# A neighbour mask and layernorm steps moved from VectorE to ScalarE in a four-layer graph kernel

## The chip, the core and the metric

The kernel runs on one core of a Trainium2 chip. A core has five engines that work side by side, each with its own list of instructions, which it takes in order: TensorE (PE; its weight loads are PEld), VectorE (DVE), ScalarE (ACT), GpSimd (POOL) and SyncE (SP). They wait for one another through semaphores. The metric is the device time of one execution in microseconds (us), the median over several runs. A profile is one execution that the hardware profiler recorded.

## The reference

Sixteen graphs of 1024 nodes with 64 features each pass through four layers. Each layer normalizes the features, clips them at zero, computes something over the graph, and adds the result to `x`:

```python
h = jnp.maximum(_layernorm(x, axis=-1), 0.0)   # (x - mean) / sqrt(var + 1e-5), per node over 64 features
x = x + layer(h, adj)                          # four times, with four different layers
```

- Layer 0: `messages = adj @ h`, then `tanh([h, messages] @ W1 + b1) @ W2 + b2`.
- Layer 1: `((adj + I) @ h) / rowsum(adj + I)`.
- Layer 2: a node's neighbours are the columns with `adj > 0`, without itself. Where there are more than ten, some are struck out by a rule on their rank. Over the neighbours that remain (and the node itself) the 25, 50 and 75% quantiles are taken in each feature, weighted 0.25, 0.5, 0.25 and added to `h`; two matrix products with a Relu follow, and the node mask.
- Layer 3: `(adj @ h) / degree @ W_n + h @ W_s + bias`.

The adjacency is not negative: an entry is zero or between 0.05 and 1.

## The kernel before

Nodes lie 128 to a tile, eight tiles to a graph (`NB = 8`, `C = 64`, `P = 128`). A graph's work is cut into six streams, Python generators that emit instructions piece by piece:

- `adjacency` (from L863): for each of eight row blocks it takes a block `a` of 128 x 1024 float32 that was loaded three blocks ahead, makes the mask `nb` (L874: 1 where `a > 0`) and clears its diagonal (L876), transposes `a` on TensorE into `adjt` (L881, copied out by ScalarE at L882), and counts the neighbours of each row on ScalarE, by a pass over `nb` with an accumulator output (L887). Then it makes keys for the neighbours that remain (L895 to L956), writes them to DRAM, and orders the nodes by their number of neighbours (L958 to L1004).
- `layers`: layers 0 and 1, and layer 2's layernorm, whose result goes to DRAM as `h_d`.
- `neighbour_lists`: the keys come back in the new order of nodes by indirect DMAs from GpSimd (L1019), and VectorE draws the neighbours' numbers out, eight at a time, with MAX8 (L1034, L1048).
- `gathers`: for each neighbour place and each block of nodes one indirect DMA from GpSimd fetches 128 rows of `h_d` (L1165), 152 a graph. The blocks form five groups with their own buffers.
- `sorts`: VectorE sorts each group's gathered rows by a network of minima and maxima (L1208), one `tensor_tensor` each, and adds up the weighted quantiles (L1229, L1231).
- `tail`: eight indirect DMAs from GpSimd (L1251) fetch the sums in the old order; then come layer 2's products and layer 3.

The order is set when the program is built. A planner keeps a `Clock` with an estimated time for VectorE, TensorE, ScalarE and GpSimd. Each stream advances it with the estimated costs of what it emitted (`after(dve, pe, act)`) and yields the time from which it wants to go on. The loop at the end takes the first stream in a fixed order of priority whose time has come. So the estimates decide how the streams' instructions interleave, and every engine then executes that order as it stands. A new graph's `adjacency` begins once the previous one's keys are done and `adjt` is no longer needed. A group's gathers wait until the same group of the previous graph is sorted, and the sorts wait for the gathers.

The layernorm `preln` is called four times per graph, 64 times in all: three times from `layers`, once from `tail`. It takes the sum of the 64 features on VectorE (L816), scales it to the mean (L817), subtracts it (L818), squares on ScalarE (L819), sums the squares on VectorE (L821), takes the root on ScalarE (L822) and the reciprocal on VectorE (L824), multiplies (L825), and writes the clipped result on ScalarE (L826). The operations over the features treat all eight blocks, 512 elements per partition, in one instruction. The three yields let other streams' instructions in between.

Of the kernel before, what the change touches and what calls it, by code (L numbers as in the profile page):

```python
# [7 lines left out]
F32 = mybir.dt.float32  # L8
# [5 lines left out]
AF = mybir.ActivationFunctionType  # L14
ALU = mybir.AluOpType
AX = mybir.AxisListType

P = 128
C = 64
NB = 8  # L20
# [689 lines left out]
def direct_path(ctx: ExitStack, tc: tile.TileContext, t: dict, out: bass.AP, flag):  # L710
# [3 lines left out]
    nc = tc.nc  # L714
# [6 lines left out]
    nodes = ctx.enter_context(tc.tile_pool(name="nodes", bufs=2))  # L721
# [6 lines left out]
    tt, ts, act = nc.vector.tensor_tensor, nc.vector.tensor_scalar, nc.scalar.activation  # L728
# [55 lines left out]
    clk = Clock()  # L784

    def after(dve=0.0, pe=0.0, act=0.0, lat=0.3):

        clk.dve += dve
        at = clk.dve
        if pe:  # L790
            clk.pe = at = max(clk.pe, at) + pe
        if act:
            clk.act = at = max(clk.act, at) + act
        return at + lat


    def bank(dt=F32):
        return psum.tile([P, 2048 // mybir.dt.size(dt)], dt, tag="t", name="pt", bufs=3)
# [8 lines left out]
    def mid(u, shape):  # L807

        return work.tile(shape, F32, tag=f"mid{u}", name="mid", bufs=2)

    def preln(u, x, ha):

        s = nodes.tile([P, 4, NB], F32, name="stat")
        xc = mid(u, [P, NB, C])
        sq = mid(u, [P, NB, C])
        nc.vector.tensor_reduce(s[:, 0], x, AX.X, ALU.add)  # L816
        ts(s[:, 1], s[:, 0], 1.0 / C, None, op0=ALU.mult)  # L817
        tt(xc, x, s[:, 1, :, None].to_broadcast([P, NB, C]), ALU.subtract)  # L818
        act(sq, xc, AF.Square)  # L819
        yield after(1.5, act=0.65)  # L820
        nc.vector.tensor_reduce(s[:, 2], sq, AX.X, ALU.add)  # L821
        act(s[:, 3], s[:, 2], AF.Sqrt, bias=eps, scale=1.0 / C)  # L822
        yield after(0.7, act=1.0)
        nc.vector.reciprocal(s[:, 2], s[:, 3])  # L824
        tt(xc, xc, s[:, 2, :, None].to_broadcast([P, NB, C]), ALU.mult)  # L825
        act(ha[:, :, :C], xc, AF.Relu)  # L826
        yield after(0.9, act=0.65)

    def transposed(h, dst):

# [28 lines left out]
    def load_rows(k):  # L859

        if k < B * NB:
            a = loads.tile([P, N], F32, name="a", bufs=3)
            nc.sync.dma_start(a, adj[k // NB, k % NB * P:(k % NB + 1) * P, :])  # L863
            queued.append(a)


    def adjacency(b):
        g = state[b]
        adjt = graph.tile([P, NB, N], F32, name="adjt")
        nb = graph.tile([P, NB, N], F16, name="nb")  # L870
        mn = nodes.tile([P, 3, NB], F32, name="mn")
        for i in range(NB):
            a = queued.pop(0)
            ts(nb[:, i, :], a, 0.0, None, op0=ALU.is_gt)  # L874
            d = slice(i * P, (i + 1) * P)
            tt(nb[:, i, d], nb[:, i, d], offdiag, ALU.mult)  # L876
            for q in range(2):
                p = bank()
                for u in range(4):
                    j = 4 * q + u  # L880
                    nc.tensor.transpose(p[:, u * P:(u + 1) * P], a[:, j * P:(j + 1) * P], identf)  # L881
                nc.scalar.copy(adjt[:, 4 * q:4 * q + 4, i * P:(i + 1) * P],  # L882
                               p.rearrange("p (u m) -> p u m", m=P))
            load_rows(NB * b + i + 3)
            for q in range(2):
                s = slice(q * 512, (q + 1) * 512)
                act(nb[:, i, s], nb[:, i, s], AF.Copy, accum_out=mn[:, q, i:i + 1])  # L887
            yield max(after(0.9, pe=2.2, act=2.9) - 3.0, clk.dve + 3.1)
        g.update(adjt=adjt, at=clk.act)
        done.add(("rows", b))  # L890

# [24 lines left out]
        for i in range(NB):  # L916
# [8 lines left out]
            for q in range(2):  # L925
                s = slice(q * 512, (q + 1) * 512)
# [3 lines left out]
            if waiting:  # L930
                yield waiting[2]
                ts(gone[:, waiting[0], :], waiting[1], sf[:, 1, waiting[0]:waiting[0] + 1], -1.0,  # L932
                   op0=ALU.is_equal, op1=ALU.mult)
# [4 lines left out]
           op0=ALU.is_equal, op1=ALU.mult)  # L938
# [3 lines left out]
        for i in range(NB):  # L942

            p = bank2()
            for q in range(2):
                s = slice(q * 512, (q + 1) * 512)
# [143 lines left out]
    def layers(b):  # L1090
# [4 lines left out]
        yield max(g["at"], clk.dve + 3)  # L1095
        ha = nodes.tile([P, NB, C + 1], F32, name="ha")
        yield from preln(0, x, ha)
        zt = big(0, [P, N])
        transposed(ha, zt[:C])
# [11 lines left out]
        clk.dve += 0.7  # L1111
        ha = nodes.tile([P, NB, C + 1], F32, name="ha")
        yield from preln(0, x, ha)

        nc.vector.memset(ha[:, :, C:], 1.0)  # L1115
# [23 lines left out]
        clk.dve += 2.4  # L1139
        ha = nodes.tile([P, NB, C + 1], F32, name="h2", bufs=3)  # L1140
        yield from preln(0, x, ha)
        nc.sync.dma_start(h_ds[b % 3][:N].rearrange("(i p) c -> p i c", p=P), ha[:, :, :C])
        ts(deg[:, 1], deg[:, 0], 0.0, None, op0=ALU.is_equal)
# [178 lines left out]
    def over_graphs(step, *needs):  # L1322
# [5 lines left out]

    streams = [
        over_graphs(adjacency, ("adjt", 1), ("keys", 1), ("sorts", 3)),  # L1330
        over_graphs(layers, ("rows", 0), ("tail", 3)),
        over_graphs(tail, ("sorts", 0)),
# [142 lines left out]
```

## Time and profile before

| | before |
|---|---|
| time, median of 3 runs | 5551.11 us (5551.11 to 5564.75) |
| span of the profiled execution | 4044.6 us |
| VectorE busy | 3476.7 us, 86% of the span |
| GpSimd busy | 2951.5 us, 73% |
| TensorE busy | 2039.3 us, 50% |
| ScalarE busy | 1411.8 us, 35% |
| granted TensorE clock | 0.698 of full speed |

The profiled execution is shorter than the timed ones by 1507 us, although the program and its inputs are the same. So the profile shows in which way the engines wait for one another, while its lengths can't simply be carried over to the timed runs.

In the profile, "busy" is the time in which an engine executes an instruction that isn't mere control. A group's line gives the source line, the engine, the operation, what is written and read, the number of instructions, the busy time in us and the mean of one in ns, and behind the second bar the idle time of the engine just ahead of these instructions with what ended it. "issue" there means that the profile shows nothing that the engine waited for.

### The profile page before, as it was taken

How to read it: one execution, taken by the hardware profiler on the slowest of the kernel's cores; microseconds unless marked ns; L12 is line 12 of the kernel's file. 1: busy time of each engine (PE TensorE's matmuls, PEld its weight loads, DVE VectorE, ACT ScalarE, POOL GpSimd, SP SyncE). 2: the span in 40 equal slices, each digit the busy share in tenths (PEclk: the TensorE clock that was granted, in tenths of full speed). 3: DMA queues.
4: the chain of work that ended last, by engine and by line, in shares of the span. 5: the costliest groups of instructions: out<-in, count | busy, mean ns of one | idle time of the engine just before them, and what ended most of it. 6: DMA issues, size and time to landing. Idle time of an engine off the chain costs nothing.

```text
span 4044.6 us, 34028 instructions
## 1 busy us (share of the span) xinstructions
PE 2039.3 (50%) x8387; PEld 980.5 (24%) x8387; DVE 3476.7 (86%) x9450; ACT 1411.8 (35%) x2594; POOL 2951.5 (73%) x2707
## 2 busy tenths in 40 slices
PE   7565574264735546473554647455454745540303
PEld 3223231121313122231322213132221313110101
DVE  2649998997999999998998989899998999997583
ACT  6544442342425333342533434253432424320000
POOL 0277777777777777777777777777777777777771
PEclk8676676576767767776675767677677776765656
DMA  2343543444434454543444444443535444442312
GB/s 88 115 87 88 120 111 53 110 92 90 117 55 126 86 120 94 109 104 50 125 90 115 94 96 114 53 138 74 130 83 105 108 62 112 76 109 37 68 26 53
DMA packets 251857, 372.57 MB, mean 92 GB/s; under 512 B 120160, under 2 KB 120352, under 8 KB 251648
## 3 DMA queue, kind: packets, MB, share of 16 engines
q0 software_dynamic: 92640, 117.88, 23.5%
q1 hardware_dynamic: 158864, 251.87, 18.4%
q8 instruction: 68, 1.11, 0.1%
q14 instruction: 141, 1.16, 0.1%
q10 hardware_dynamic: 144, 0.56, 0.0%
HBM read 256.84 MB, written 113.25 MB: 92 GB/s over the span
## 4 chain that ended last, share of the span: by engine, by line
POOL 41%; DVE 33%; issue 13%; PE 5%; DMA 5%; ACT 2%; DVEq 0%; POOLq 0%; ACTq 0%
POOL raw L1165 37%; DVE other L1208 8%; DVE raw L1208 7%; DVE most L1048 5%; PE pt L845 4%; POOL res L1251 3%; DMA raw<-h_d,index 2%; DVE found L1034 2%; DVE agg L1231 2%; DVE k L1045 1%; DMA k<-keys_d,node 1%; DVE found L1050 1%; DVE k L1043 1%; ACT adjt L1125 1%; DVE nb L874 1%
## 5 line engine op out<-in xcount | busy, mean ns | idle before, releaser
L1165 POOL DMA_INDIRECT raw<-h_d,index x2432 | 2666.0, 1096 | 757.5 <-issue 724.7
L1208 DVE TENSOR_TENSOR other<-raw 128x128 f32<-128x128 f32 (+7 forms) x1488 | 766.5, 533 | 73.4 <-DMA raw<-h_d,index 60.3
L1208 DVE TENSOR_TENSOR raw<-other 128x256 f32<-128x256 f32 (+10 forms) x1424 | 679.1, 490 | 4.3
L845 PE MATMUL pt<-adjt,ha 128*65 128x512 f32 (+1 forms) x1024 | 492.9, 644 | 299.3 <-DVE ha L1115 299.2
L881 PE MATMUL pt<-ef,a 128*128 128x128 f32 x1024 | 232.7, 391 | 389.4 <-ACT adjt L882 354.5
L1295 PE MATMUL tm<-at,ha 128*64 128x512 f32 x512 | 286.0, 677 | 54.9 <-DMA at<-adjt_d 52.4
L845 PEld LDWEIGHTS pt<-adjt,ha 128*65 128x65 f32 (+1 forms) x1024 | 150.0, 150 | 621.9 <-issue 569.6
L1048 DVE MAX8 most<-k 128x8 uint16<-128x1024 uint16 x224 | 275.0, 1228 | 7.7
L881 PEld LDWEIGHTS pt<-ef,a 128*128 128x128 f32 x1024 | 173.5, 203 | 441.8 <-ACT adjt L882 391.0
L922 PE MATMUL pt<-eh,nbt 128*128 128x512 f16 (+3 forms) x1024 | 210.0, 364 | 125.9 <-ACT nbt L911 125.4
L1019 POOL DMA_INDIRECT k<-keys_d,node x128 | 131.0, 1023 | 191.2 <-DVE node L1004 122.0
L956 ACT ACTIVATE nb<-pt 128x1024 f16<-128x1024 f32 x128 | 130.8, 1022 | 390.2 <-PE pt L952 248.3
L834 PE MATMUL pt<-ef,res 128*64 128x128 f32 x128 | 30.2, 418 | 425.7 <-DVE res L1255 335.3
L1034 DVE MAX8 found<-k 128x8 f32<-128x1024 f16 x128 | 156.3, 1221 | 99.2 <-DMA k<-keys_d,node 99.2
L887 ACT ACTIVATE nb<-nb 128x512 f16<-128x512 f16 x256 | 159.6, 628 | 206.2 <-DVE nb L876 119.4
L978 ACT ACTIVATE sink<-pt,neg 128x1024 f16<-128x1024 f32 x128 | 140.4, 1121 | 244.9 <-PE pt L973 244.9
L1208 DVE TENSOR_TENSOR other<-raw,other 128x256 f32<-128x256 f32 (+4 forms) x592 | 206.9, 354 | 5.4
L846 ACT COPY big<-pt 64x1024 f32<-64x1024 f32 (+1 forms) x32 | 32.2, 1007 | 505.9 <-PE pt L845 505.9
L1251 POOL DMA_INDIRECT res<-agg_d,pos x128 | 146.1, 1141 | 83.5 <-DMA agg_d<-agg 43.0
L927 ACT ACTIVATE ab<-pt,sf 128x512 f16<-128x512 f32 x256 | 161.8, 687 | 124.6 <-DVE gone L932 67.8
L1208 DVE TENSOR_TENSOR raw<-raw,other 128x256 f32<-128x256 f32 (+3 forms) x608 | 203.0, 338 | 0.0
L1208 DVE TENSOR_TENSOR raw<-other,raw 128x128 f32<-128x128 f32 (+5 forms) x560 | 196.1, 357 | 3.1
(154 smaller groups left out, 4068.0 us busy)
## 6 DMA issues: line engine op xcount, KB each, us to landing
a<-in_adj_dram SPq DMA_DIRECT2D x128, 512.0 KB, 3.6
adjt_d<-adjt SPq DMA_DIRECT2D x128, 512.0 KB, 5.7
at<-adjt_d SPq DMA_DIRECT2D x256, 256.0 KB, 3.8
raw<-h_d,index POOLq DMA_INDIRECT x2432
keys_d<-nb SPq DMA_DIRECT2D x128, 256.0 KB, 2.3
x<-in_x_dram SPq DMA_DIRECT2D x16, 256.0 KB, 2.9
h_d<-h SPq DMA_DIRECT2D x16, 256.0 KB, 4.2
agg_d<-agg SPq DMA_DIRECT2D x16, 256.0 KB, 2.8
```

Source lines behind the costliest of these rows:

```text
L845: nc.tensor.matmul(p[p0:p0 + n, s], h[:, j, :n], adjt[:, j, s], start=j == 0, stop=j == NB - 1)
L881: nc.tensor.transpose(p[:, u * P:(u + 1) * P], a[:, j * P:(j + 1) * P], identf)
L887: act(nb[:, i, s], nb[:, i, s], AF.Copy, accum_out=mn[:, q, i:i + 1])
L922: nc.tensor.matmul(p[:, o:e], nbt[:, j, :], stair[:, :e - o], start=j % 4 == 0, stop=j % 4 == 3)
L927: act(ab[:, s], p[:, s], AF.Abs, bias=sf[:, 2 + q, i:i + 1], scale=2.0)
L978: act(sink, p, AF.Sign, bias=neg[:, i:i + 1], accum_out=over[:, i:i + 1])
L1034: nc.vector.max(out=found[:, o:o + 8], in_=src)
L1048: nc.vector.max(out=most, in_=less.bitcast(U16))
L1165: nc.gpsimd.indirect_dma_start(raw[:, s, i * C:(i + 1) * C], None, h_ds[b % 3], bass.IndirectOffsetOnAxis(ap=g["index"][:, at:at + 1], axi ...
L1208: tt(to, v0, v1, ALU.max if greater else ALU.min)
L1251: nc.gpsimd.indirect_dma_start(res[:, i, :], None, g["agg_d"], bass.IndirectOffsetOnAxis(ap=g["pos"][:, i:i + 1], axis=0))
L1295: nc.tensor.matmul(p[:C, :], ha[:, j, :C], ats[k], start=j == 0, stop=j == NB - 1)
```

## The change

The mask is made by ScalarE's `Sign` in place of VectorE's comparison. The row sums are taken with `Relu` in place of `Copy`, so that an entry below zero, of which `Sign` makes -1, counts as no neighbour. In the layernorm the mean's negative goes as a bias column into ScalarE's `Square`, and the sum of squares comes out of the same instruction's accumulator; the last step is one `Relu` with a scale and a bias column. A column is one value per partition, so each of these becomes eight instructions of 64 elements, one per block of nodes. The subtraction, the second reduction and the multiplication over 512 elements leave VectorE; a product of eight elements is added. The planner's costs and two of its due times are set anew. The aim is to take work off VectorE.

```diff
     def preln(u, x, ha):
-        s = nodes.tile([P, 4, NB], F32, name="stat")
-        xc = mid(u, [P, NB, C])
+        s = nodes.tile([P, 5, NB], F32, name="stat")
         sq = mid(u, [P, NB, C])
         nc.vector.tensor_reduce(s[:, 0], x, AX.X, ALU.add)
-        ts(s[:, 1], s[:, 0], 1.0 / C, None, op0=ALU.mult)
-        tt(xc, x, s[:, 1, :, None].to_broadcast([P, NB, C]), ALU.subtract)
-        act(sq, xc, AF.Square)
-        yield after(1.5, act=0.65)
-        nc.vector.tensor_reduce(s[:, 2], sq, AX.X, ALU.add)
+        ts(s[:, 1], s[:, 0], -1.0 / C, None, op0=ALU.mult)
+        for i in range(NB):
+            act(sq[:, i], x[:, i], AF.Square, bias=s[:, 1, i:i + 1], accum_out=s[:, 2, i:i + 1])
         act(s[:, 3], s[:, 2], AF.Sqrt, bias=eps, scale=1.0 / C)
-        yield after(0.7, act=1.0)
+        yield after(0.8, act=4.3)
         nc.vector.reciprocal(s[:, 2], s[:, 3])
-        tt(xc, xc, s[:, 2, :, None].to_broadcast([P, NB, C]), ALU.mult)
-        act(ha[:, :, :C], xc, AF.Relu)
-        yield after(0.9, act=0.65)
+        tt(s[:, 4], s[:, 1], s[:, 2], ALU.mult)
+        for i in range(NB):
+            act(ha[:, i, :C], x[:, i], AF.Relu, bias=s[:, 4, i:i + 1], scale=s[:, 2, i:i + 1])
+        yield after(0.2, act=2.0)
...
     def adjacency(b):
...
             a = queued.pop(0)
-            ts(nb[:, i, :], a, 0.0, None, op0=ALU.is_gt)
+            act(nb[:, i, :], a, AF.Sign)
             d = slice(i * P, (i + 1) * P)
             tt(nb[:, i, d], nb[:, i, d], offdiag, ALU.mult)
...
-                act(nb[:, i, s], nb[:, i, s], AF.Copy, accum_out=mn[:, q, i:i + 1])
-            yield max(after(0.9, pe=2.2, act=2.9) - 3.0, clk.dve + 3.1)
+                act(nb[:, i, s], nb[:, i, s], AF.Relu, accum_out=mn[:, q, i:i + 1])
+            yield max(after(0.2, pe=2.2, act=3.9) - 4.0, clk.dve + 3.1)
```

## The prediction

> **What bounds the kernel now.** I read the page from the top. Parts 1 and 2 give the engines' busy time and its course over the span:
>
> ```profile
> PE 2039.3 (50%) x8387; PEld 980.5 (24%) x8387; DVE 3476.7 (86%) x9450; ACT 1411.8 (35%) x2594; POOL 2951.5 (73%) x2707
> ...
> DVE  2649998997999999998998989899998999997583
> ...
> POOL 0277777777777777777777777777777777777771
> ```
>
> DVE has the larger share, but POOL is the flat row: 7 in every slice but the ends. A flat 7 is either an engine that is held up by the same thing all the time, or one that is full with a fixed gap per instruction. The group of L1165 (the row gathers) and that line's own answer say which:
>
> ```profile
> L1165 POOL DMA_INDIRECT raw<-h_d,index x2432 | 2666.0, 1096 | 757.5 <-issue 724.7 <-DVE s L1060 15.7 <-DMA raw<-h_d,index 12.8
> ```
>
> ```profile
> L1165 POOL DMA_INDIRECT raw<-h_d,index x2432: 940/965/5474, 188.7 to 3953.1; - x188
> ...
>   issue: 724.7, 2378
> ```
>
> Of 757.5 us of idle time before the gathers, 724.7 is "issue": 0.30 us ahead of nearly each one, in which GpSimd waits for nobody. So a gather costs 1.096 + 0.30 = 1.40 us, and with the key and result gathers there are 2688: 2688 x 1.40 = 3763 us, and from the first raw gather (188.7) to the last (3953.1) there are 3764 us. GpSimd is full. DVE keeps pace beside it and isn't what the gathers wait for (a few tens of us in all).
>
> The second thing is the spread, 940 to 5474 ns with a median of 965. The timeline around the longest one shows why:
>
> ```profile
> 748.90 5.47 POOL L1165 DMA_INDIRECT raw<-h_d,index  x1 [0.30 <-issue]
> 748.97 0.42 DVE L1208 TENSOR_TENSOR other<-raw,other 128x256 f32<-128x256 f32 x1
> 749.30 0.42 DVE L1208 TENSOR_TENSOR raw<-other,raw 128x256 f32<-128x256 f32 x1
> ...
> 754.26 0.28 DVE L1208 TENSOR_TENSOR other<-raw 128x128 f32<-128x128 f32 x1
> ```
>
> Sort steps with two SBUF inputs run one into the next, and the gather stands until the row of them has a gap. I sorted all 2688 gathers by what DVE did during each, from the trace's starts and durations: DVE idle, 214 gathers, mean 0.944 us; MAX8 alone, 78, 0.944; MAX8 and operations with one input, 340, 0.959; two-input operations alone, 1380, 1.131 and up to 5.47; L874 with two-input operations, 122, 1.238; L874 with MAX8 and other one-input operations, 3, 0.945. So two-input DVE operations hold the gather up and one-input ones hardly do, L874 included as far as three cases can tell. The sum over 0.94 us is 416 us.
>
> **The timed runs.** They take 5551 us, the profiled execution 4044.6. The program and the data are the same, so something that the trace shows only weakly costs 1507 us more. The hold-up above fits: without a record per instruction DVE would leave fewer gaps, and the gathers would stand longer. The sum: unhindered gathers 2688 x (0.944 + 0.30) = 3344 us. The ends: 135 us until the first key gather, 41 us of waiting from there to 188.7 (54 less ten gathers at 1.24), 28 us between the last raw gather and the first result gather, 56 us after the last: 260. In the profile 3344 + 260 + 416 = 4020 of 4044.6, so the account closes. For the timed run 5551 - 3344 - 260 = 1947 us of hold-up are left. DVE's operations with two SBUF inputs, each counted to the start of the next, are 1922 us at L1208, 301 at L1231 and 287 elsewhere: 2510. So the timed run would hold GpSimd up for 1947 / 2510 = 0.78 us per us of such operations. That is an inference; no view of a timed run exists. If it holds, DVE is idle for 5551 - 3477 = 2074 us there, and only its two-input time counts.
>
> **What the Trainium skill says.** "SBUF — State Buffer", section "SBUF: two separate sides", says that VectorE and GpSimd share one pair of SBUF ports, an exclusive lock for the whole instruction, which a VectorE operation with two SBUF inputs also takes against a GpSimd operation that reads SBUF. The 5.47 us gather agrees. The page counts the fast one-input modes among the blockers too; the trace shows little of that (0.959 against 0.944). "DMA: Bandwidth & Descriptors", section "SWDGE vs HWDGE vs iDMA", says that GpSimd itself writes the descriptors of its DMAs into rings in SBUF, which is why a gather, though a DMA, can be held up so. "ScalarE: Activation LUTs", section "What ACT_TABLE_LOAD costs", prices an ACTIVATE at 186 ns + 0.833 ns per element, 93 ns more per pointer operand, with 93 ns of overlap. The trace agrees: 371 ns for 104 elements with one pointer (L1078; formula 366), 300 ns for 8 (L822; 286).
>
> **The change part by part.** The rows that carry the prices:
>
> ```profile
> L874 DVE TENSOR_SCALAR nb<-a 128x1024 f16<-128x1024 f32 x128 | 88.4, 691 | 18.3 <-DMA a<-in_adj_dram 18.1 <-issue 0.2
> L825 DVE TENSOR_TENSOR mid<-mid,stat 128x512 f32<-128x512 f32 x64 | 44.6, 696 | 2.3
> L818 DVE TENSOR_TENSOR mid<-x,stat 128x512 f32<-128x512 f32 x64 | 44.3, 692 | 2.2
> L821 DVE TENSOR_REDUCE stat<-mid 128x8 f32<-128x512 f32 x64 | 43.4, 678 | 18.2 <-ACT mid L819 18.1
> L819 ACT ACTIVATE mid<-mid 128x512 f32<-128x512 f32 x64 | 40.6, 634 | 255.2 <-DVE mid L818 255.2
> L956 ACT ACTIVATE nb<-pt 128x1024 f16<-128x1024 f32 x128 | 130.8, 1022 | 390.2 <-PE pt L952 248.3 <-PE pt L955 141.9
> L887 ACT ACTIVATION_READ_ACCUMULATOR nb<-nb 128x1 f32 x256 | 49.4, 193 | 0.0
> ```
>
> *Layernorm, 64 times.* DVE loses L818, L821 and L825, which take 0.63, 0.60 and 0.62 us to the start of the next operation, and gains one product of 8 elements (0.17, as L1147): 1.68 us less each, 108 in all. Of this the two-input part is 40.1 + 39.5 - 64 x 0.17 = 69 us. ACT loses two passes of 0.63 us and gains eight squares of 64 elements with a bias pointer, 333 - 93 = 240 ns each, plus an accumulator read of 193 ns less about 90 of overlap: 0.34 x 8 = 2.7 us; and eight Relus with two pointers, 426 - 93 = 333 ns: 2.7 us. That is some 4.3 us more per layernorm, 275 in all.
>
> *Mask, 128 times.* DVE loses 0.69 us, 88 us in all, one-input. ACT gains a Sign over 1024 elements: 1.02 us as L956, 0.93 back to back, 119 us. Relu for Copy in the row sums costs the same. Sign, Square and Relu run in the trace without a table load of their own, so I add no loads. ACT goes from 1412 to about 1800 us, still far from full.
>
> *The new wait.* L876 on DVE now follows the Sign at once. I put the Sign ahead of each row's L882 copies in ACT's order and took when ACT came free there: in most rows ACT is 1 to 3 us early; behind the tail's Relus (L1263) it is 4 to 7 us late. Over graphs 1 to 15 this comes to some 140 us of DVE standing, with the sort steps queued behind it, against 108 + 88 = 196 us saved. Nobody waits for that DVE time while gathers are what is short, and a standing DVE lets a gather through. Layernorm itself gets longer: at the end L818's start to L826's end is 4.0 us (4003.1 to 4007.1), and becomes about 6.2.
>
> *The ends.* Nothing hides ACT there. In graph 0 ACT is full over the rows (2.2 us a row): 7 x 0.93 = 6.5 us; two layernorms beside the keys' ACT work add some 5.5 together (between 0 and 8.6); the last layernorm adds 2. Sum +14 us.
>
> *Sum.* -69 x 0.78 = -53, +14: -39 us. 5551 - 39 = 5512 us. The bounds: no hold-up removed gives 5565; all 69 us gives 5496; with L874 as a full blocker too, (69 + 88) x 0.78 = 122 less 14: 5443.
>
> **The rivals.**
> 1. *The hold-up isn't what the timed run adds* (GpSimd is slower there by itself): only the ends count, 5551 + 14 = 5565, no change. For it: nothing of the timed run is seen. Against: 5.47 us gathers beside unbroken two-input rows, none beside MAX8.
> 2. *DVE is the bound in the timed run*: 196 us off in full, plus the ends, 5551 - 196 + 14 = 5369. For it: 86% busy, and the chain passes through DVE for 33%. Against: GpSimd without a wait through the whole middle.
> 3. *Slower.* The chain from rows over keys and lists to the next gathers gets longer: 8.7 us of standing per graph for the Sign, plus three layernorms of the layers at 2.2 us, less 5.5 us of mask: about 9.8 x 16 = 157 us; were all of it to reach the gathers, 5551 + 157 - 39 = 5669. The planner also reorders everything after its new costs, and longer unbroken sort rows would hold gathers longer. Against: the raw gathers waited for DVE for some 20 us in the whole profile, and come later still in the timed run.
>
> **How the numbers follow.** Forecast 0.50, rival 1 0.18, rival 2 0.12, rival 3 0.20. Predicted: 5512. The range 5400 to 5610 takes in the forecast with its bounds, rival 1, and the halves of rivals 2 and 3 that are nearer. Under 5534 is faster by over 0.3%: most of the forecast (0.46) and rival 2 make 0.58. Same: rival 1 and the forecast's upper edge, 0.20. Slower: rival 3 and the part of rival 1 whose ends cost more than 17 us, 0.22.
>
> **What would show it.** In the changed profile: DVE busy near 3290 us, ACT near 1800, table loads still 33, GpSimd's issue still 0.30 us per gather, and the gathers' mean a little under 1096 ns. L876 should show tens of us of waiting for ACT, L1165 hardly any for DVE. First key gather near 147 us instead of 135. I am wrong if the gathers begin to wait for DVE or for lists, or if the time falls by about the whole DVE saving.

## The result, and the profile after

The changed kernel takes 5734.23 us (median of 4 runs, 5706.27 to 5765.19); the kernel before is put beside it at 5557.93 us (median of 4 runs, 5551.11 to 5579.64, three of which are those of the table above). The ratio is 1.031, with a 95% interval of 1.025 to 1.037: 176 us slower, where 39 us faster was forecast, and outside the range of 5400 to 5610.

One fact about these numbers has to come first. In all later comparisons the same kernel before took 4043 to 4057 us, like its first profile, and the changed kernel 4068 us. So the first comparison was made in surroundings (whatever lies outside the program) that cost both kernels some 1500 us. What they were, no run here shows. The record puts the later comparisons on three chips (numbers 9, 14 and 7) and doesn't name the chip of the first. The granted TensorE clock in the changed kernel's runs was lower in the first, 0.62 to 0.63 of full speed against 0.68 to 0.69 later, but TensorE's busy time is only 3% longer there (2122.8 against 2053.8 us), so that isn't where 1500 us go. The profile of the changed kernel is itself one of the four timed executions (5706.27 us), so for once it can be seen where the time goes. Parts 1, 2 and 4 of its page:

```profile
PE 2122.8 (37%) x8387; PEld 1007.6 (18%) x8387; DVE 3304.6 (58%) x9194; ACT 1809.7 (32%) x4130; POOL 2716.7 (48%) x2707
...
DVE  1348546576576738557393755728467374863545
...
POOL 0425551726447472625637263562626537265440
...
DVE 38%; another core or an unknown queue 28%; issue 11%; ACT 10%; PE 9%; DMA 2%; POOL 1%; DVEq 0%; SPq 0%; ACTq 0%; POOLq 0%
```

No engine is full, and GpSimd's flat row of 7 has gone: it works and waits by turns. 28% of the chain, 1596 us, are waits for which the profile names no releaser. The groups of the gathers of rows and of keys (busy us, mean ns, idle us before with what ended it):

```profile
L1163 POOL DMA_INDIRECT raw<-h_d,index x2432 | 2421.3, 996 | 1009.5 <-issue 731.4
L1017 POOL DMA_INDIRECT k<-keys_d,node x128 | 145.8, 1139 | 1448.3 <-DVE node L1002 1084.6
```

A row gather takes 0.996 us, less than in the profile before (1.096), where the forecast's sum for the timed runs makes 1.67 (0.944 and 1947 us over 2688 gathers). GpSimd isn't held up longer; it waits 1085 us for the ordered nodes that the next graph's keys need. Three of the longer waits of the other engines (total, times, longest, in us):

```profile
ACT nbt L909 <- remote: 536.9, 37, 31.0
DVE gone L930 <- ACT ab L925: 457.2, 25, 102.3
DVE nb L874 <- ACT nb L872: 165.0, 28, 26.2
```

The new wait for the Sign is there (L874 for L872), 165 us. But hardly any of the 102 us before one L930 is work. The timeline from 284 us on, inside that wait, where GpSimd gathers without a pause:

```profile
284.70 0.94 POOL L1163 DMA_INDIRECT raw<-h_d,index  x1 [0.30 <-issue]
284.82 0.27 PE L908 MATMUL pt<-eh,nb 128*128 128x128 f16 x1 [2.56 <-issue]
285.95 0.94 POOL L1163 DMA_INDIRECT raw<-h_d,index  x1 [0.30 <-issue]
286.22 0.10 PEld L908 LDWEIGHTS <-nb 128*128 128x128 f16 x1 [2.72 <-issue]
287.20 0.95 POOL L1163 DMA_INDIRECT raw<-h_d,index  x1 [0.30 <-issue]
287.62 0.27 PE L908 MATMUL pt<-eh,nb 128*128 128x128 f16 x1 [2.53 <-issue]
```

TensorE's weight loads and products start 1.40 us apart here, though they take 0.10 and 0.27 us and wait for nothing on record: 2.8 us for one transpose. In 126 of the 128 rows of this trace a whole set of eight takes under 1 us from the first start to the last.

And finished work is told late. L843 ends at 280.2 us; ScalarE, which has nothing else to do, copies its result out 76 us later:

```profile
279.19 1.01 PE L843 MATMUL pt<-adjt,ha 128*64 128x512 f32 x1 [1.79 <-issue]
356.24 1.01 ACT L844 COPY big<-pt 64x1024 f32<-64x1024 f32 x1 [77.85 <-remote]
```

The trace also keeps the times at which semaphores were raised. TensorE finished three pieces of work that raise its semaphore, at 280.2, 301.9 and 324.3 us; the three updates stand at 356.22, 356.31 and 356.40, after the last gather of the stretch (339.4), and ScalarE starts 0.02 us after the first. Over the execution 544 of the 7116 updates by TensorE, VectorE and ScalarE come more than 1 us after the end of the last instruction that makes one, counted so by up to 62 us; in the same kernel's later profile (e4 below) 6 of 8655 do, and the median delay is 8 to 14 ns in both. 466 of the 544 belong to instructions that ended while gathers ran with less than 1 us between them. All of the 1596 us without a releaser are waits for semaphores of these three engines, 1326 of them for TensorE's; at least 1325 of the 1596 us pass after the last instruction that raises the awaited semaphore has ended. So most of this share of the chain is late word of finished work. The counts are rough, since this profile lacks about 1500 of these updates. What delays them, no run shows.

The stretches of the page's windows show what that leaves of the engines (busy us of each in the stretch):

```profile
201.00:300.00 99.00, 38.16 (x103) 12.59 (x101) 6.42 (x25) 17.32 (x45) 74.41 (x79) 0.60 0.31 26
300.00:360.00 60.00, 5.34 (x15) 1.77 (x16) 0.49 (x1) 3.19 (x4) 29.98 (x32) 0.50 0.15 18
360.00:448.00 88.00, 49.36 (x208) 19.99 (x205) 80.20 (x271) 52.75 (x118) 0.00 (x0) 0.73 0.20 75
```

The columns are PE, PEld, DVE, ACT, POOL. In this first stretch, up to 360 us, VectorE works 7 us in 159; in the 88 us without gathers that follow, 80. Not every stretch is as slow: added up over the execution, those with gathers less than 1 us apart take 3507 us with VectorE 48% busy, the rest 2197 us with 73%. In these surroundings the gathers and the other engines' work stand partly in line, one behind the other.

### The profile page after: what moved, and what is told of

Its sections match the earlier page's. It is cut to its first block, busy times and chain, and to the rows that moved or that the text cites. A ratio compares the mean times of both kernels' runs of the same rounds, so it can differ in the third digit from the quotient of the medians.

```text
span 5704.4 us, 35484 instructions
## 1 busy us (share of the span) xinstructions
PE 2122.8 (37%) x8387; PEld 1007.6 (18%) x8387; DVE 3304.6 (58%) x9194; ACT 1809.7 (32%) x4130; POOL 2716.7 (48%) x2707
## 4 chain that ended last, share of the span: by engine, by line
DVE 38%; another core or an unknown queue 28%; issue 11%; ACT 10%; PE 9%; DMA 2%; POOL 1%; DVEq 0%; SPq 0%; ACTq 0%; POOLq 0%
DVE other L1206 11%; DVE raw L1206 10%; DVE most L1046 3%; DVE agg L1229 3%; PE pt L843 3%; ACT sink L976 2%; DVE found L1032 2%; ACT mid L818 1%; DVE half L1229 1%; ACT nb L885 1%; PE tm L1293 1%; ACT nb L872 1%; ACT ha L824 1%; DVE k L1043 1%
## 5 line engine op out<-in xcount | busy, mean ns | idle before, releaser
L1163 POOL DMA_INDIRECT raw<-h_d,index x2432 | 2421.3, 996 | 1009.5 <-issue 731.4
L1017 POOL DMA_INDIRECT k<-keys_d,node x128 | 145.8, 1139 | 1448.3 <-DVE node L1002 1084.6
L920 PE MATMUL pt<-eh,nbt 128*128 128x512 f16 (+3 forms) x1024 | 236.7, 393 | 1041.5 <-issue 569.2
L843 PE MATMUL pt<-adjt,ha 128*65 128x512 f32 (+1 forms) x1024 | 505.9, 653 | 300.1 <-DVE ha L1113 223.4
L1293 PE MATMUL tm<-at,ha 128*64 128x512 f32 x512 | 310.1, 731 | 268.9 <-DMA at<-adjt_d 185.2
L930 DVE TENSOR_SCALAR gone<-ab,sf 128x1024 f16<-128x1024 f16 x112 | 55.1, 493 | 600.5 <-ACT ab L925 457.2
L909 ACT COPY nbt<-pt 128x1024 f16<-128x1024 f16 x128 | 128.8, 1009 | 660.5 <-remote 536.9
L920 PEld LDWEIGHTS <-nbt 128*128 128x128 f16 x1024 | 111.3, 123 | 1161.7 <-issue 650.2
L818 ACT ACTIVATE mid<-x,stat 128x64 f32<-128x64 f32 x512 | 170.6, 337 | 336.3 <-DVE stat L816 139.1
L843 PEld LDWEIGHTS pt<-adjt,ha 128*65 128x65 f32 (+1 forms) x1024 | 151.0, 151 | 633.5 <-issue 563.4
L880 ACT COPY adjt<-pt 128x512 f32<-128x512 f32 x256 | 137.4, 581 | 386.9 <-remote 302.1
```

The costliest lines, as they stand in the source:

```text
L818: act(sq[:, i], x[:, i], AF.Square, bias=s[:, 1, i:i + 1], accum_out=s[:, 2, i:i + 1])
L843: nc.tensor.matmul(p[p0:p0 + n, s], h[:, j, :n], adjt[:, j, s], start=j == 0, stop=j == NB - 1)
L920: nc.tensor.matmul(p[:, o:e], nbt[:, j, :], stair[:, :e - o], start=j % 4 == 0, stop=j % 4 == 3)
L1017: nc.gpsimd.indirect_dma_start(k, None, g["keys_d"], bass.IndirectOffsetOnAxis(ap=g["node"][:, i:i + 1], axis=0))
L1163: nc.gpsimd.indirect_dma_start(raw[:, s, i * C:(i + 1) * C], None, h_ds[b % 3], bass.IndirectOffsetOnAxis(ap=g["index"][:, at:at + 1], axi ...
L1293: nc.tensor.matmul(p[:C, :], ha[:, j, :C], ats[k], start=j == 0, stop=j == NB - 1)
```

## The experiments

**A second profile of the kernel before.** No edit.

> The kernel before, unchanged, for a second profile of it. The first profile's span (4045 us) does not go with the timed 5551 us. If the timed executions go the way of the first profile and GpSimd is only held up longer by VectorE (the forecast's inference), this span is either 4045 again or near 5551 with raw gathers of about 2 us each and GpSimd without waits. If instead the timed executions have waits that the first profile lacks (as the changed kernel's profile has: 1085 us of GpSimd waiting for the ordered nodes, 1500 us of chain in waits that no record explains), the span is near 5551 with gathers of about 0.95 to 1.0 us and long waits of GpSimd.

Measured: 4057.65 us, span 4055.7. Its row-gather group:

```profile
L1165 POOL DMA_INDIRECT raw<-h_d,index x2432 | 2674.0, 1100 | 757.8 <-issue 724.0 <-DVE s L1060 15.8 <-DMA raw<-h_d,index 14.7
```

It is the first profile again: GpSimd full, hardly a wait. So 4045 us isn't a freak of one profiled execution (15 timed runs beside it took 4033 to 4059 us); the 5558 us were those of the first comparison. The waits without a releaser were not met again, so the second half of the question has no answer for the kernel before.

**The mask alone, and layernorm alone.**

```diff
# e2: mask as changed, preln as before
-            ts(nb[:, i, :], a, 0.0, None, op0=ALU.is_gt)
+            act(nb[:, i, :], a, AF.Sign)
# e3: preln as changed, mask as before
+            act(sq[:, i], x[:, i], AF.Square, bias=s[:, 1, i:i + 1], accum_out=s[:, 2, i:i + 1])
+            act(ha[:, i, :C], x[:, i], AF.Relu, bias=s[:, 4, i:i + 1], scale=s[:, 2, i:i + 1])
```

> Only the mask's part of the change, with its planner costs; layernorm as before. Theory A (the wait for the Sign is what costs): all or most of the 176 us, 5690 to 5740. Theory B (the longer layernorm chain costs): near before, 5540 to 5580. Theory C (the order that the planner's new costs make): in between or anywhere, and the two parts need not add up.

> Only layernorm's part of the change, with its planner costs; the mask as before. Theory A: near before, 5540 to 5580. Theory B: most of the 176 us, 5680 to 5740. Theory C: anywhere, and this and the mask alone need not add up to 176 us.

Measured beside before at 4043.32 us: the mask 4041.45 us, ratio 0.9996 (0.9981 to 1.0011); layernorm 4074.0 us, 1.0087 (1.0058 to 1.0117). The absolute times of the expectations belong to the first comparison and don't apply. The mask takes 86 us off VectorE (3391.6 against 3477.7 in e1), puts 108 us of waiting for the Sign on it, and comes to nothing. Layernorm takes 114 us off VectorE (3363.7) and loses 0.9%.

**The whole change again, and its operations under the old planner costs.**

```diff
# e5 against the changed kernel
-        yield after(0.8, act=4.3)
+        yield after(2.2, act=1.65)
-        yield after(0.2, act=2.0)
+        yield after(0.9, act=0.65)
-            yield max(after(0.2, pe=2.2, act=3.9) - 4.0, clk.dve + 3.1)
+            yield max(after(0.9, pe=2.2, act=2.9) - 3.0, clk.dve + 3.1)
```

> The changed kernel once more, beside runs of the kernel before, which took 4043 us in the experiments so far where it took 5558 us beside the changed kernel's first runs. The parts gave 0.9996 and 1.0087. If the parts add up: ratio 1.005 to 1.012, some 4060 to 4090 us, gathers at about 1.09 us and back to back. If the loss of 3.1% is the change's in any surroundings (the wait for the Sign and the longer layernorm together): ratio 1.025 or more, over 4145 us. If the first profile's unexplained waits are the kernel's own, they are here again and the span is near 5700; if they are those of the surroundings, they are gone.

> The changed kernel's operations with the planner costs of before: after(2.2, act=1.65) and after(0.9, act=0.65) in layernorm, after(0.9, pe=2.2, act=2.9) - 3.0 in the mask. If the operations themselves cost the time (longer layernorm on ScalarE, the wait for the Sign): as e4 or slower, since the plan then underrates ScalarE. If the planner's new costs and the order that they make cost it: near 1.000, faster than e4.

Measured beside before at 4053.22 us: the changed kernel 4068.43 us, ratio 1.0033 (1.0017 to 1.0049); with the old costs 4051.54 us, 0.9988 (0.9975 to 1.0001). The page of the changed kernel (e4), parts 1 and 2, and its row gathers:

```profile
PE 2053.8 (51%) x8387; PEld 993.4 (24%) x8387; DVE 3275.8 (81%) x9194; ACT 1801.8 (44%) x4130; POOL 2919.1 (72%) x2707
...
DVE  1559699699878889898888998888888888896582
...
POOL 0177677677777777777777777777777777777771
...
L1163 POOL DMA_INDIRECT raw<-h_d,index x2432 | 2637.8, 1085 | 760.9 <-issue 719.8 <-DMA raw<-h_d,index 23.5 <-DVE s L1058 14.5
```

Neither the sum of the parts nor the 3.1% came back. The waits without a releaser are gone, so they are no property of the kernel alone: each of the compute engines executes the same instructions in the same order in both traces, and up to 200 us their starts lie within about 3 us of each other. They part where the first back-to-back row gathers begin. VectorE has 202 us less to do than in e1, and GpSimd is as full as before. The parts (0.9996 and 1.0087) don't add up to the whole (1.0033), and the planner's costs alone are worth 0.45% (e4 against e5): the order that they make counts for more than the operations do, which under the old costs change nothing clear of noise.

**The ends.**

```diff
# e6: e5, and the old operations where no other work hides ScalarE
+            if b: act(nb[:, i, :], a, AF.Sign)
+            else: ts(nb[:, i, :], a, 0.0, None, op0=ALU.is_gt)
-        yield from preln(0, x, ha)
+        yield from (preln if b else preln_old)(0, x, ha)
-        yield from preln(1, x, ha)
+        yield from (preln if b + 1 < B else preln_old)(1, x, ha)
```

> The changed kernel with the planner costs of before (as e5, which gave 0.9988), and at the two ends the old operations: graph 0's mask and its three layernorms, and the last graph's tail layernorm, as before. If the forecast's term for the ends is right (+14 us, with nothing beside it to hide ScalarE), this is some 14 us under e5: ratio 0.994 to 0.997. If the ends are not where the change loses: 0.998 to 1.000.

Measured: 4043.78 us, ratio 0.9975 (0.9964 to 0.9986), 0.13% or 5 us under e5, not 14. The intervals of the two overlap, so a cost of the ends isn't clear of the noise, while 14 us (0.35%) would be. In the traces the first row gather comes 7 us earlier than in e5 (187.4 against 194.1) and the part after the last is 1 us shorter. This version has the lowest ratio here, 0.25% under before.

**Which VectorE time counts.**

```diff
# e7, after the diagonal is cleared in each mask row of the kernel before
+            for _ in range(6):
+                tt(junk, a[:, :192], a[:, 512:704], ALU.add)
# e8, in its place
+            for _ in range(6):
+                nc.vector.tensor_reduce(junk[:, :3], a[:, :192].rearrange("p (g c) -> p g c", c=64), AX.X, ALU.add)
```

> The kernel before, with six additions of two 128x192 SBUF operands into a tile that nobody reads after each mask row (768 in all, about 0.27 us each: some 207 us more of VectorE). Not part of the reference. If two-input operations hold the gathers up as the first profile suggests (416 us for 2510, 0.17 us per us), the hold-up grows by some 35 us, and the time exceeds that of e8 by as much: ratio 1.008 to 1.02 with e8 lower. If VectorE's load alone counts, e7 and e8 are alike. If the hold-up were 0.78 per us, as the forecast took for the timed runs: +160 us, 1.04.

> As e7, with six sums over one 128x192 operand in place of the six additions: the same load on VectorE, one SBUF input. Not part of the reference. If only two-input operations hold gathers up: near before, 1.000 to 1.008, gathers' mean no longer than in e1. If VectorE's load counts: like e7.

Measured beside before at 4057.18 us: 4222.11 us, ratio 1.0408 (1.0383 to 1.0433), and 4217.25 us, 1.0397 (1.0375 to 1.042). Both expectations that rested on the hold-up missed. e7 alone would look like a hit for 0.78 us per us (+160 us, 1.04), but e8 costs the same with one input, so that agreement is chance. Two inputs or one make no difference, and the gathers don't get longer (sum over 0.944 us: 390 and 400 us, 415 in e1). The time goes into GpSimd's waits for the nodes and keys, in e7 first, then in e1:

```profile
L1022 POOL DMA_INDIRECT k<-keys_d,node x128 | 150.1, 1173 | 369.7 <-DVE node L1007 213.9 <-DVE found L1053 76.8 <-DVE other L1211 24.3
L879 DVE TENSOR_TENSOR junk<-a 128x192 f32<-128x192 f32 x768 | 275.5, 359 | 22.1
```

```profile
L1019 POOL DMA_INDIRECT k<-keys_d,node x128 | 128.6, 1004 | 196.2 <-DVE node L1004 127.2 <-DVE found L1050 33.9 <-issue 26.2
```

The added operations took 0.36 us each (0.35 in e8) rather than 0.27: VectorE's busy time rises from 3477.7 us (e1) to 3742.6. These 265 us put in cost 165 us; 202 us taken out (e4) gain nothing. Between 400 and 3600 us VectorE is 95% busy in e7, 92% in e1 and 87% in e4. This fits a VectorE just under GpSimd: more load on it soon sets the time, less meets GpSimd's floor. But the additions stand in the mask rows, ahead of the keys, so e7 and e8 don't tell VectorE's load as such from a longer path to the next keys; no run has the same load elsewhere.

**More instructions on ScalarE, twice.**

```diff
         act(ha[:, :, :C], xc, AF.Relu)
+        for i in range(23):
+            act(junk[:, i:i + 1], eps, AF.Copy)
```

> The kernel before, with 23 copies of one column on ScalarE after each layernorm (1472 in all, as many instructions as the change adds on ScalarE), which nobody waits for; not part of the reference. If in the surroundings of the first comparison (before at 5558 us) the time goes with the number of instructions, and these surroundings come back: about 1.03 or more. If the surroundings are those of e1 to e5 (before near 4045 us), ScalarE's load and the number of instructions should cost nothing: 0.998 to 1.003; over 1.005 would mean that work queued on ScalarE is itself a part of the change's cost.

> The kernel of e9 (before with 1472 more instructions on ScalarE that nobody waits for) once more, to meet the surroundings of the first comparison. If before runs near 5558 us beside it: 1.03 says that the number of instructions costs there, 1.00 that it does not and that the change's longer chain does. If before runs near 4050 us again: 1.000 as e9, and the cause of the first comparison's 3.1% stays open.

Measured: 4060.58 us beside 4057.18, ratio 1.0009 (0.9999 to 1.0019), and in the second comparison 4044.98 beside 4043.38, 0.9998 (0.9984 to 1.0013). 1472 more instructions and 130 us more of ScalarE cost nothing where before takes 4050 us. The surroundings of the first comparison didn't come back, so whether the number of instructions counts there stays open.

## Why the prediction was wrong

**The step that failed is the paragraph on the timed runs.** It saw that the profile's 4044.6 us and the timed 5551 us don't go together, and closed the gap by an inference: 1947 us of longer hold-up, 0.78 us per us of two-input VectorE time. The changed kernel's profile in the same surroundings shows the opposite: gathers of 0.996 us, with 171 us in all over 0.944, while GpSimd stands idle for 2609 us between the first and the last row gather, against 839 in e1. So what that execution spends its time on is the chain of work that feeds GpSimd, 1325 us of it at least waits for word of work that was done, and the only gain of the forecast (69 us x 0.78 = 53) had no object. Nor was it the records that the timed runs lacked, as the paragraph had it: this profile has a record per instruction and is one of the slow timed runs. The view from the first profile, in which way the engines wait for one another, didn't carry over either. The inference was called one, but it carried the direction, and no rival let the gap be late signals between the engines; rival 1 dropped the hold-up but had GpSimd itself slower. That the account closed for the profile said nothing for the timed runs. It also closes a little less well than it says: the hold-up is summed over 0.94 us and the floor taken at 0.944, so that it is 406 us and the sum 4010 of 4044.6.

**The hold-up itself was mis-sized too.** In the trace it stands beside two-input rows, and from e1 to e4 it does fall, from 415 to 373 us. But e2, which takes only one-input operations off VectorE, has 396, e5 with e4's operations in another order has 354, and adding two-input operations in e7 left it at 390. So it is no price per us of two-input operations. What the Trainium skill says of the shared port pair ("SBUF — State Buffer", section "SBUF: two separate sides") may be what holds single gathers; no run here shows that it sets the time of the kernel.

**The prices held.** VectorE 3276 us in e4 (forecast near 3290), ScalarE 1802 (near 1800), no added table loads. The rows of e4:

```profile
L818 ACT ACTIVATE mid<-x,stat 128x64 f32<-128x64 f32 x512 | 170.4, 336 | 336.1 <-DVE stat L816 336.0
L872 ACT ACTIVATE nb<-a 128x1024 f16<-128x1024 f32 x128 | 134.2, 1049 | 4.9 <-DMA a<-in_adj_dram 4.6
L824 ACT ACTIVATE ha<-x,stat 128x64 f32<-128x64 f32 x384 | 132.6, 440 | 47.1 <-DVE stat L822 47.1
L874 DVE TENSOR_TENSOR nb<-nb,eh 128x128 f16<-128x128 f16 x128 | 28.5, 223 | 195.3 <-ACT nb L872 192.0 <-DMA adjt_d<-adjt 2.9
```

A Square was put at 333 ns and takes 336, a Relu with two pointers at 426 and takes 440, the Sign at 1022 and takes 1049. So the formula of the Trainium skill's page "ScalarE: Activation LUTs", section "What ACT_TABLE_LOAD costs", held for columns within 3%. The forecast's terms for ScalarE in a layernorm make 4.1 us, not the 4.3 that it wrote, and 4.1 is what e3 shows (264.6 us in 64). The wait for the Sign was put at 140 us and is 192.

**The ends** were put at +14 us. From e1 to e4 the first key gather comes 16 us later (138.3 to 154.2; forecast 12), but the first row gather only 7 (192.0 to 199.2), since the lists behind it run faster; from the last row gather to the end it is 91.7 and 93.1 us. Together 8.6 us, and 5 by the difference of e5 and e6, which isn't clear of the noise.

**Where the 202 us went where before takes 4050 us.** The stretch between the first and the last row gather lasts 3772.0 us in e1 and 3771.7 in e4. In it the gathers got shorter by 39 us in all (2933.4 to 2894.6), and GpSimd's idle time grew by 39 (838.6 to 877.1). What VectorE no longer does it mostly spends waiting: 192 us for the Sign, and 197 us for gathered rows ahead of sort steps, 61 in e1. The forecast's view that GpSimd is the floor and that nobody waits for the saved VectorE time was right for the profile that it was read from.

**Rival 3 had the side**: a longer chain from rows over keys to the next gathers, put at 5669, 118 us slower. Without the forecast's gain of 53 its 157 us and the ends make 171, near the 176 measured, but it counted no late signals, so the nearness proves nothing. GpSimd's 1085 us of waiting for the nodes fits it. It isn't shown. No profile of the kernel before from those surroundings exists, and the extra instructions (35484 records against 34028) are a second candidate that no run could test there. Rival 2, VectorE as the bound, is refuted by e4 for the later surroundings: 202 us off in full, and none of it in the time. In the first comparison's own profile VectorE is 58% busy. Rival 1 named the right number for the later surroundings (the ends only, +14 us; e4 is 15 over before), though not for its reason, since the ends are about half of that.

What stays open: what the surroundings of the first comparison were, what delayed the signals in them, and which part of the change costs the 3.1% there, or whether the change does at all, as both kernels were never met in them again.

## What to carry to other kernels

If a profile's span and the timed runs differ by a third, the profile isn't of what is being timed: a forecast should then be split over both cases, not carried from one into the other by a fitted factor. Where a profile names no releaser for a wait, set the semaphores' update times beside the ends of the instructions that raise them: here the work had long been done. Beside a full engine, time taken off the next one brings nothing: 202 us less on VectorE left the time as it was, though 265 us more, put ahead of the keys, cost 165. And where a planner orders the work, its costs are part of the change; the same operations under the old costs took 0.45% less time.

## What the runs showed of the hardware

The same program took 4068 us in some surroundings and 5734 in others, with every engine's instructions in the same order. In the slower ones the engines' semaphore updates came up to 76 us after the work was done, mostly while GpSimd issued row gathers back to back (466 of the 544 late ones counted); in e4 they came after some 10 ns, gathers or not. In four stretches, some 115 us in all, TensorE's instructions also started 1.40 us apart whatever their length (0.10 to 1.01 us); in e4 none do. With gathers under way VectorE is 48% busy in the slower profile and 85% in e4, and the gathers themselves take about 1 us in both (0.996 and 1.085). As the program is the same, what differs lies outside it.
